# Value product of two local-attention models with the values as the loaded operand

## The chip, the cores and the metric

The kernel runs on one core of one Trainium2 chip. The metric is the device time of one execution in microseconds, as the median of the runs shown. The core has TensorE (PE, whose weight loads are shown apart as PEld), VectorE (DVE), ScalarE (ACT), GpSimd (POOL) and SyncE (SP), which issues the DMAs.

## The reference, cut to what matters

The network is a chain of four parts: a chunked attention, a first local-attention model (six layers, 16 heads, window 32), a causal linear attention, and a second local-attention model (two layers, 8 heads, window 64), each with its normalisations and residuals. The change touches the local attention, which both models share. Per head, with w the window and 64 features:

```python
bq = q.reshape(b, h, nw, w, d)
bk2, bv2 = (look(bk), look(bv))        # own window and the one before: 2w keys
sim = jnp.einsum('bhwie,bhwje->bhwij', bq, bk2) * QK_SCALE
sim = jnp.where(mask, -jnp.finfo(sim.dtype).max, sim)
attn = jax.nn.softmax(sim, -1)
out = jnp.einsum('bhwij,bhwje->bhwie', attn, bv2)
...
return out @ Wo
```

Everything is computed in fp32. There are 4096 tokens of width 128 (two batches of 2048).

## The kernel before, in words

After a first stage of about 600 us (the chunked attention, `l0_attention`), `local_models` runs both local models as one sequence of tiles. A tile is 128 tokens of one batch in one layer: 6 layers x 32 = 192 tiles of the first model (W = 32, four windows to a tile, 16 heads), then 2 x 32 = 64 of the second (W = 64, two windows, 8 heads). The linear attention lies beside the last layers as small steps (`lsteps`), and each layer's feed-forward as steps of 512 tokens (`steps`).

The loop at line 1471 is a software pipeline written out by hand. Each engine executes its instructions in the order of this loop. In iteration i, with j = i + 3:

1. `scores(i+1)` (line 974), then the exponential and the row sums (`weights_exp`, `weights_norm`),
2. `project(j, 0)` (line 862): queries and keys by TensorE (L871), squares on ACT (L873), rotary products on DVE (L881, L886) with a sum on POOL (L892), and in the last unit the norms on DVE (L897 and `rsqrt_quick`, ending in rq_y at L180) and two scalings on POOL (L904),
3. a feed-forward step, then `keys_first_(i)` (line 1023), which transposes the attention weights to pT (keys on partitions; L1030, copied by ACT at L1031), then the rest of the projection,
4. `mix(i)` (line 1034): the value product (L1047), copied by ACT to `on` (L1053),
5. `values(i+2)` (line 943): the values by TensorE (L955), copied by ACT (L956), and DMAs that lay them out as v2 with 2W keys on partitions,
6. `turn_out(i)` (line 1056): `on` is transposed by TensorE (L1063) and copied by ACT to oT (L1064), which has features on partitions,
7. `turn(i+2)` (L936): queries and keys are transposed,
8. a feed-forward step, then `project_out(i)` (line 1067): oT times Wo (L1075), and the residual by DVE (L1081).

PSUM is held as two buffers of two banks (`wide`: projection and scores) and a ring of four single banks (`bank`: everything else). The scratch of `rsqrt_quick` lies in the projection's own PSUM buffer, so that this buffer comes free when rq_y is done.

The small products of scores and of the value product use parts of the 128x128 array. In `scores` a head's 64 features take half of the rows (q = 0 or 1 chooses the half), a window's W queries are the loaded columns, and the 2W keys are streamed. In `mix` the 2W keys of a window are the rows (half of the array for W = 32, chosen by s; all of it for W = 64), a window's W queries are the loaded columns (pT), and the 64 features of v2 are streamed; the output has queries on partitions.

The pieces of the trace are read by these line numbers. The trace has two records for each fp32 matmul and for each of its loads.

Of the kernel before, what the change touches and what calls it, by code (L numbers as in the profile page):

```python
# [11 lines left out]
F32 = mybir.dt.float32  # L12
# [60 lines left out]
def tile_kernel(ctx: ExitStack, tc: tile.TileContext, a: dict, out: bass.AP):  # L73
    nc = tc.nc
# [26 lines left out]
    def bc(ap, shape):  # L101
        return ap.to_broadcast(list(shape))

    ident = const.tile([128, 128], F32, name="ident")
# [603 lines left out]
    def local_models(mA, mB, hs0):  # L708
# [3 lines left out]
        wk = ctx2.enter_context(tc.tile_pool(name="f_k", bufs=1))  # L712
# [4 lines left out]
        def wide(name):  # L717

            return psA.tile([128, 1024], F32, tag="A", name=f"ps_{name}")

        def bank(name):
            return psT.tile([128, 512], F32, tag="T", name=f"ps_{name}")
# [50 lines left out]
        layers = [(m, l) for m in models for l in range(m.depth)]  # L773
        tiles = [(g, b, t) for g in range(len(layers)) for t in range(NTILE) for b in range(B)]
        n, per = len(tiles), B * NTILE
        st = [dict() for _ in range(n)]
# [4 lines left out]
        def load_proj(g, u):  # L781

            m, l = layers[g]
            w = wpool.tile([128, 1024], F32, tag="wp", name="wp", bufs=4)
            c = u * 1024
            k = min(1024, 3 * m.INNER - c)
            nc.sync.dma_start(w[:, 0:k], a[f"{m.pre}_ffn_Wqkv"][l, :, c:c + k])
            wts[g, u] = w
# [185 lines left out]
        def scores(i):  # L974

            g, b, t = tiles[i]
            m, _ = layers[g]
            W, H, HPG = m.W, m.H, m.HPG
            qT, kT = st[i].pop("q"), st[i].pop("k")
            sp = wide("s")  # L980
            for q in range(2):


                rows, sel, j = (slice(0, 128), identb, 0) if t == 0 else (
                    slice(64 * q, 64 * q + 64), pick, 1)
                nc.tensor.matmul(
                    sp[:, 512 * q:512 * q + 512], lhsT=sel[rows],
                    rhs=bc(m.maskb[rows, j].unsqueeze(1), (rows.stop - rows.start, HPG, 2 * W)),
                    start=True, stop=False,
                )  # L990
            for cc in range(HPG):
                for q in range(2):
                    for w in range(m.NW):
                        c0 = 512 * q + 2 * W * cc
                        nc.tensor.matmul(  # L995
                            sp[W * w:W * w + W, c0:c0 + 2 * W],
                            lhsT=qT[64 * q:64 * q + 64, cc, W * w:W * w + W],
                            rhs=kT[64 * q:64 * q + 64, cc, W * w:W * w + 2 * W],
                            start=False, stop=(cc == HPG - 1),
                        )  # L1000
            v = lambda x: x.rearrange("p (h k) -> p h k", k=2 * W)
            mx = wk.tile([128, 16], F32, name="mx")
            nc.vector.tensor_reduce(mx[:, 0:H], v(sp), AX.X, ALU.max)  # L1003
            sm = wk.tile([128, 1024], F32, name="sm", bufs=2)
            nc.vector.tensor_tensor(
                v(sm), v(sp), bc(mx[:, 0:H].unsqueeze(2), (128, H, 2 * W)), ALU.subtract
            )
            st[i]["p"] = sm

        def weights_exp(i):  # L1010
            sm = st[i]["p"]
            nc.scalar.activation(sm, sm, AF.Exp)  # L1012

        def weights_norm(i):
            m, _ = layers[tiles[i][0]]
            sm = st[i]["p"]
            v = sm.rearrange("p (h k) -> p h k", k=2 * m.W)
            rs = wk.tile([128, 16], F32, name="rs", bufs=2)[:, 0:m.H]
            nc.vector.tensor_reduce(rs, v, AX.X, ALU.add)  # L1019
            nc.vector.reciprocal(rs, rs)  # L1020
            nc.gpsimd.tensor_tensor(v, v, bc(rs.unsqueeze(2), (128, m.H, 2 * m.W)), ALU.mult)  # L1021
# [11 lines left out]

        def mix(i):

            m, _ = layers[tiles[i][0]]
            W, NO = m.W, m.NO
            pT, v2 = st[i].pop("pT"), st[i].pop("v")
            po = [bank("o") for _ in range(NO)]
            on = wk.tile([128, 2, 4, 128], F32, name="on")  # L1040
            for c in range(4):
                for s in range(NO):
                    kp = slice(2 * W * s, 2 * W * (s + 1))
                    for q in range(2):
                        co = 128 * c + 64 * q
                        for w in range(m.NW):
                            nc.tensor.matmul(  # L1047
                                po[s][W * w:W * w + W, co:co + 64],
                                lhsT=pT[kp, q, c, W * w:W * w + W],
                                rhs=v2[kp, w, co:co + 64], start=True, stop=True,  # L1050
                            )
            for s in range(NO):
                nc.scalar.copy(on[:, s].rearrange("p c i -> p (c i)"), po[s])  # L1053
            st[i]["on"] = on

        def turn_out(i):
            m, _ = layers[tiles[i][0]]
            on = st[i].pop("on")
            oT = wk.tile([128, 2, 4, 128], F32, tag="pT", name="oT")
            for s in range(m.NO):  # L1060
                p = bank("oT")
                for c in range(4):
                    nc.tensor.transpose(p[:, c * 128:(c + 1) * 128], on[:, s, c, :], ident)  # L1063
                nc.scalar.copy(oT[:, s].rearrange("p c i -> p (c i)"), p)  # L1064
            st[i]["o"] = oT

        def project_out(i):
# [21 lines left out]
        def step():  # L1089
            if steps:  # L1090
                steps.pop(0)()
# [4 lines left out]
        def lstep():  # L1096
            if lsteps:
                lsteps.pop(0)()
# [372 lines left out]
        for i in range(-3, n):  # L1471
            j = i + 3
            lstep()
            if 0 <= i + 1 < n:
                scores(i + 1)
                weights_exp(i + 1)
                weights_norm(i + 1)
            more = False
            if j < n:
                g, b, t = tiles[j]  # L1480
                jj = j % per
                nu = len(layers[g][0].units)
                more = g < last
                if g == second and t % 4 == 0:
                    while (b, t // 4) not in ready:
                        lstep()
                if nu == 2:
                    project(j, 0)
                if more and jj == 4:
                    load_proj(g + 1, 0)  # L1490
                if more and jj == 6 and g + 1 == second:
                    models[1].consts()
                if jj == 6 and g == second - 1:
                    linear_consts()
                if more and jj == 8:
                    factors(g + 1)
                    if 2 == 2:
                        load_out(g + 1)
                if more and jj == 18:
                    load_ff(g + 1)  # L1500
                if more and jj == 22:
                    fold_ff(g + 1)
                if nu == 2 and more and jj == per - 1:
                    load_proj(g + 1, 1)
                lstep()
            step()
            if i >= 0:
                keys_first_(i)
            if 0 <= i + 2 < n:
                halo(i + 2)  # L1510
            if j < n:
                project(j, nu - 1)
                if nu == 2 and more and jj == per - 1 and g + 1 < second:
                    load_proj(g + 1, 2)
                if nu == 1 and more and jj == per - 1:
                    load_proj(g + 1, 1)
                if b == B - 1 and j + 1 < n:
                    tables(*tiles[j + 1][::2])
            lstep()
            if i >= 0:  # L1520
                mix(i)
            lstep()
            if 0 <= i + 2 < n:
                values(i + 2)
            lstep()
            if i >= 0:
                turn_out(i)
            if 0 <= i + 2 < n:
                for u in range(len(layers[tiles[i + 2][0]][0].units)):
                    turn(i + 2, u)  # L1530
            step()
            lstep()
            if i >= 0:
                g, b, t = tiles[i]
                project_out(i)
                if 2 == 1 and i % per == per - 1 and g < last:
                    load_out(g + 1)
                if t % 4 == 3:
                    feed_forward(g, b, t // 4)
# [74 lines left out]
```

## Time and profile before

| what | value |
|---|---|
| runs | 4997.42, 5001.14, 5006.03 us; median 5001.14 |
| the profiled execution | 5004.26 us |
| its span | 5002.5 us |
| granted TensorE clock, mean | 0.961 |
| PE matmul records / PEld records | 74820 / 74850 |
| value product L1047 | 26624 records: 24576 of form 64*32 64x64, 2048 of form 128*64 128x64 |
| scores L995 | 26624 records: 24576 of form 64*32 64x64, 2048 of form 64*64 64x128 |
| transposes of the outputs L1063 | 1792 records |

A form such as "64*32 64x64" means 64 rows and 32 loaded columns of the array, with 64 partitions and 64 columns streamed. In a group of the profile, "busy" is the time in which at least one of its instructions was in flight, followed by the mean duration of one in ns; behind the bar stands the idle time of the engine just before them, and what ended it. In the timeline a row gives the start, the length, the engine, the line, the form and the number of records. In the chain that ended last a row gives the start, the length, and what held the chain.

### The profile page before, as it was taken

Reading aid. Unit: us, or ns where it says so; the run is one execution under the profiler, and the core shown is the slowest. Engines: PE = TensorE matmul, PEld = TensorE weight load, DVE = VectorE, ACT = ScalarE, POOL = GpSimd, SP = SyncE. Lnnn points to the kernel's source line nnn. Section 1 sums busy time; section 2 is a strip of 40 time slices with the busy share of each in tenths; the row PEclk is TensorE's granted clock in tenths of the full one; section 3 lists DMA queues with packets and bytes.
Section 4 is the critical chain, followed back from the end, with each engine's and each line's share of the span. In section 5 each row is a group of like instructions: output and inputs, shape, how many; then the busy total and the mean of one; then the engine's idle time right before and its main releaser. Section 6 shows DMA issues by size and latency. Waiting matters only on the chain.

```text
span 5002.5 us, 170719 instructions
## 1 busy us (share of the span) xinstructions
PE 4572.7 (91%) x74820; PEld 3143.2 (63%) x74850; DVE 3973.1 (79%) x6840; ACT 2883.5 (58%) x4665; POOL 2780.8 (56%) x1666
## 2 busy tenths in 40 slices
PE   5667799999999999999999999999999989899897
PEld 4445566666666666666666666666666666555554
DVE  6993488888888888888888888888877777787885
ACT  3233366666666656666666666666555555565564
POOL 3332366666666666666666666666555544455452
PEclk8778899999999999999999999999999999999999
DMA  2000322222222322223222322232222211111111
GB/s 77 1 1 25 84 69 67 63 72 74 71 64 63 83 71 63 63 76 76 66 66 64 83 67 64 65 78 73 54 55 52 63 45 38 39 46 40 53 53 37
DMA packets 222487, 295.59 MB, mean 59 GB/s; under 512 B 75656, under 2 KB 95408, under 8 KB 221744
## 3 DMA queue, kind: packets, MB, share of 16 engines
q1 hardware_dynamic: 221744, 284.67, 22.0%
q8 instruction: 590, 9.67, 0.8%
q14 instruction: 153, 1.25, 0.1%
HBM read 40.98 MB, written 10.75 MB: 10 GB/s over the span
## 4 chain that ended last, share of the span: by engine, by line
PE 53%; DVE 20%; ACT 8%; POOL 5%; issue 3%; DMA 1%; SPq 0%; POOLq 0%; ACTq 0%; DVEq 0%
PE ps_qk L871 11%; PE ps_v L955 6%; PE ps_f L1158 5%; PE ps_turn L936 5%; PE ps_y L1075 5%; PE ps_o L1047 5%; PE ps_s L995 4%; DVE ps_qk L897 4%; POOL r L892 3%; DVE t L886 3%; PE ps_fy L1183 3%; PE ps_oT L1063 3%; ACT sq L873 2%; DVE r L881 2%; PE ps_pT L1030 2%
## 5 line engine op out<-in xcount | busy, mean ns | idle before, releaser
L892 POOL TENSOR_TENSOR r<-r,t 128x1024 f32<-128x1024 f32 x448 | 1061.2, 2369 | 995.9 <-DVE t L886 770.5
L904 POOL TENSOR_TENSOR r<-r,rq_y 128x1024 f32<-128x1024 f32 x448 | 844.0, 1902 | 455.9 <-DVE rq_y L180 439.2
L873 ACT ACTIVATE sq<-ps_qk 128x1024 f32<-128x1024 f32 x448 | 460.4, 1028 | 1006.4 <-PE ps_qk L871 999.9
L871 PE MATMUL ps_qk<-wp,hs 128*128 128x512 f32 x1792 | 884.4, 615 | 68.3 <-DVE rq_y L180 41.3
L881 DVE TENSOR_TENSOR r<-ps_qk,tb 128x1024 f32<-128x1024 f32 (+1 forms) x512 | 550.1, 1074 | 175.4 <-ACT sq L873 166.9
L886 DVE TENSOR_TENSOR t<-ps_qk,tb 128x1024 f32<-128x1024 f32 (+1 forms) x512 | 553.2, 1080 | 145.0 <-POOL r L892 144.5
L1021 POOL TENSOR_TENSOR sm<-sm,rs 128x1024 f32<-128x1024 f32 x256 | 487.2, 1903 | 263.3 <-DVE rs L1020 172.3
L897 DVE TENSOR_REDUCE ps_qk<-sq 128x16 f32<-128x1024 f32 x448 | 549.1, 1226 | 12.3
L1047 PEld LDWEIGHTS ps_o<-v,pT 64*32 64x32 f32 (+1 forms) x26624 | 356.8, 109 | 289.1 <-ACT pT L1031 175.7
L871 PEld LDWEIGHTS ps_qk<-wp,hs 128*128 128x128 f32 x1792 | 306.7, 191 | 326.2 <-issue 235.6
L955 PE MATMUL ps_v<-wp,hs 128*128 128x512 f32 x896 | 471.9, 639 | 1.0 <-ACT on L1053 0.6
L1047 PE MATMUL ps_o<-v,pT 64*32 64x64 f32 (+1 forms) x26624 | 418.1, 224 | 59.6 <-ACT pT L1031 32.7
L1075 PEld LDWEIGHTS ps_y<-oT,wo 128*128 128x128 f32 x3584 | 429.2, 192 | 48.0 <-issue 42.2
L936 PE MATMUL ps_turn<-ident,r 128*128 128x128 f32 x3584 | 443.2, 276 | 13.3 <-POOL r L904 11.8
L1075 PE MATMUL ps_y<-oT,wo 128*128 128x128 f32 x3584 | 446.3, 276 | 1.8 <-ACT oT L1064 1.8
L936 PEld LDWEIGHTS ps_turn<-ident,r 128*128 128x128 f32 x3584 | 405.7, 143 | 19.8 <-POOL r L904 16.6
L1003 DVE TENSOR_REDUCE mx<-ps_s 128x16 f32<-128x1024 f32 (+1 forms) x256 | 312.9, 1222 | 110.8 <-PE ps_s L995 107.4
L995 PE MATMUL ps_s<-kT,qT 64*32 64x64 f32 (+1 forms) x26624 | 371.6, 230 | 0.4
L1019 DVE TENSOR_REDUCE rs<-sm 128x16 f32<-128x1024 f32 (+1 forms) x256 | 310.3, 1212 | 68.6 <-ACT sm L1012 67.5
L1158 PE MATMUL ps_f<-fx,w 128*128 128x512 f32 (+1 forms) x768 | 356.4, 600 | 1.7 <-DVE fx L1141 1.7
L995 PEld LDWEIGHTS ps_s<-kT,qT 64*32 64x32 f32 (+1 forms) x26624 | 321.3, 107 | 57.1 <-issue 46.2
L956 ACT COPY vn<-ps_v 128x512 f32<-128x512 f32 x448 | 262.5, 586 | 112.3 <-PE ps_v L955 93.4
(268 smaller groups left out, 7554.6 us busy)
## 6 DMA issues: line engine op xcount, KB each, us to landing
v<-vn SPq DMA_DIRECT2D x1276, 128.0 KB
v<-vn SPq DMA_DIRECT2D x744, 64.0 KB
v<-vn SPq DMA_DIRECT2D x64, 256.0 KB
wp<-in_L_ffn_Wqkv SPq DMA_DIRECT2D x20, 512.0 KB
xD<-xb SPq DMA_DIRECT2D x24, 256.0 KB
xb<-xD SPq DMA_DIRECT2D x24, 256.0 KB
cs<-in_cos SPq DMA_DIRECT2D x128, 32.0 KB
cs<-in_sin SPq DMA_DIRECT2D x128, 32.0 KB
```

What stands on the lines that cost most here:

```text
L871: nc.tensor.matmul(pq[:, js], lhsT=hw, rhs=wts[g, u][:, js], start=True, stop=True)
L881: nc.vector.tensor_tensor(r[:, es].rearrange("p (h d) -> p h d", d=DH), pq[:, es].rearrange("p (h d) -> p h d", d=DH), bc(tb[:, 0, s].unsq ...
L886: nc.vector.tensor_tensor(t2[:, es].rearrange("p (h s d) -> p h s d", s=2, d=32), pq[:, es].rearrange("p (h s d) -> p h s d", s=2, d=32)[: ...
L892: nc.gpsimd.tensor_tensor(r, r, t2, ALU.add)
L897: nc.vector.tensor_reduce(pq[:, 16 * v:16 * v + 16], st[i].pop(("sq", v)).rearrange("p (h d) -> p h d", d=DH), AX.X, ALU.add,)
L904: nc.gpsimd.tensor_tensor(rv, rv, bc(y[:, 16 * v:16 * v + 16].unsqueeze(2), (128, 16, DH)), ALU.mult)
L936: nc.tensor.transpose(p[:, c * 128:(c + 1) * 128], r[:, cs], ident)
L955: nc.tensor.matmul(p, lhsT=hw, rhs=wv, start=True, stop=True)
L995: nc.tensor.matmul(sp[W * w:W * w + W, c0:c0 + 2 * W], lhsT=qT[64 * q:64 * q + 64, cc, W * w:W * w + W], rhs=kT[64 * q:64 * q + 64, cc, W ...
L1047: nc.tensor.matmul(po[s][W * w:W * w + W, co:co + 64], lhsT=pT[kp, q, c, W * w:W * w + W], rhs=v2[kp, w, co:co + 64], start=True, stop=True,)
L1075: nc.tensor.matmul(py[:, 0:128], lhsT=wts[g, "o"][:, c * NO + s, :], rhs=oT[:, s, c, :], start=(c + s == 0), stop=(c == 3 and s == NO - 1),)
L1158: nc.tensor.matmul(ps_[c][0:sz], lhsT=wts[g, "w1"][:, o:o + sz], rhs=S["x"], start=True, stop=True,)
```

## The change

In `mix` the two operands change places: the values (v2, 2W keys by 64 features) are loaded, and the attention weights (pT, 2W keys by W queries) are streamed. The output then has features on partitions: the two heads of a pair (q) go to the two column halves of the array, and the result is what `turn_out` made. `turn_out` and its call are removed, and the copy by ACT writes oT, which gets a buffer of its own in place of `on` (before, it shared pT's). The loops are ordered so that, for W = 32, consecutive matmuls go to the four quarters of the array in turn (s the row half, q the column half). In `scores` the two inner loops change places, so that consecutive matmuls alternate between the row halves.

```diff
--- before.py
+++ after.py
@@ -989,8 +989,8 @@
                     start=True, stop=False,
                 )
             for cc in range(HPG):
-                for q in range(2):
-                    for w in range(m.NW):
+                for w in range(m.NW):
+                    for q in range(2):
                         c0 = 512 * q + 2 * W * cc
                         nc.tensor.matmul(
                             sp[W * w:W * w + W, c0:c0 + 2 * W],
@@ -1033,35 +1033,25 @@
 
         def mix(i):
 
+
             m, _ = layers[tiles[i][0]]
             W, NO = m.W, m.NO
             pT, v2 = st[i].pop("pT"), st[i].pop("v")
             po = [bank("o") for _ in range(NO)]
-            on = wk.tile([128, 2, 4, 128], F32, name="on")
+            oT = wk.tile([128, 2, 4, 128], F32, name="oT")
             for c in range(4):
-                for s in range(NO):
-                    kp = slice(2 * W * s, 2 * W * (s + 1))
+                for w in range(m.NW):
                     for q in range(2):
                         co = 128 * c + 64 * q
-                        for w in range(m.NW):
+                        for s in range(NO):
+                            kp = slice(2 * W * s, 2 * W * (s + 1))
                             nc.tensor.matmul(
-                                po[s][W * w:W * w + W, co:co + 64],
-                                lhsT=pT[kp, q, c, W * w:W * w + W],
-                                rhs=v2[kp, w, co:co + 64], start=True, stop=True,
+                                po[s][64 * q:64 * q + 64, 128 * c + W * w:128 * c + W * w + W],
+                                lhsT=v2[kp, w, co:co + 64],
+                                rhs=pT[kp, q, c, W * w:W * w + W], start=True, stop=True,
                             )
             for s in range(NO):
-                nc.scalar.copy(on[:, s].rearrange("p c i -> p (c i)"), po[s])
-            st[i]["on"] = on
-
-        def turn_out(i):
-            m, _ = layers[tiles[i][0]]
-            on = st[i].pop("on")
-            oT = wk.tile([128, 2, 4, 128], F32, tag="pT", name="oT")
-            for s in range(m.NO):
-                p = bank("oT")
-                for c in range(4):
-                    nc.tensor.transpose(p[:, c * 128:(c + 1) * 128], on[:, s, c, :], ident)
-                nc.scalar.copy(oT[:, s].rearrange("p c i -> p (c i)"), p)
+                nc.scalar.copy(oT[:, s].rearrange("p c i -> p (c i)"), po[s])
             st[i]["o"] = oT
 
         def project_out(i):
@@ -1523,8 +1513,6 @@
             if 0 <= i + 2 < n:
                 values(i + 2)
             lstep()
-            if i >= 0:
-                turn_out(i)
             if 0 <= i + 2 < n:
                 for u in range(len(layers[tiles[i + 2][0]][0].units)):
                     turn(i + 2, u)
```

## The prediction

> **What bounds the kernel now.** I read the page's busy line first, then the busy times by stage, the chain that ended last, the groups of the lines that the change edits, and last the instruction timeline, for the pace of TensorE inside each edited stage.
>
> ```profile
> PE 4572.7 (91%) x74820; PEld 3143.2 (63%) x74850; DVE 3973.1 (79%) x6840; ACT 2883.5 (58%) x4665; POOL 2780.8 (56%) x1666
> ...
> PE 53%; DVE 20%; ACT 8%; POOL 5%; issue 3%; DMA 1%; SPq 0%; POOLq 0%; ACTq 0%; DVEq 0%
> ```
>
> ```profile
> core 0: us, PE busy (x) PEld busy (x) DVE busy (x) ACT busy (x) POOL busy (x), PEclk, DMA share, GB/s
> 606.00:4007.00 3401.00, 3292.01 (x62588) 2280.70 (x62590) 2816.40 (x4561) 2121.08 (x3400) 2137.28 (x1249) 0.99 0.27 68
> 4021.00:4950.00 929.00, 835.42 (x7404) 546.60 (x7404) 720.73 (x1520) 542.62 (x820) 451.41 (x291) 0.97 0.16 44
> ```
>
> The two windows run from the first to the last scores matmul of the first local model (192 tiles, 17.8 us each) and of the second (64 tiles). In the first PE is busy 97% and DVE 83%; in the second 90% and 78%. Summing the chain in slices of 100 us, PE holds 2104 of 3217 us (65%) up to 3820 us and 528 of 1179 us (45%) after it. So PE work is the first bound of the first model, and a shared one in the second. This is a stretch of that chain in which only PE works:
>
> ```profile
> 2451.36 1.72 PE ps_qk L871 x4
> 2453.08 1.50 PE ps_o L1047 x104
> 2454.59 1.91 PE ps_v L955 x4
> 2456.50 0.87 PE ps_oT L1063 x8
> 2457.37 1.75 PE ps_turn L936 x16
> ```
>
> Elsewhere the chain leaves PE for a loop: projection L871 (2.0 us), square on ACT (1.0), then on DVE, POOL and DVE again up to rq_y, whose end frees the two-bank buffer for the next projection. One such loop took 15.3 us (2409.62 to 2424.94), some 2 us under a tile's average.
>
> **Pace of the edited stages.** The timeline of PE shows each as a burst; records overlap, so the pace is (bar length less one record) / (records less one).
>
> ```profile
> 2453.01 1.58 PE L1047 MATMUL ps_o<-v,pT 64*32 64x64 f32 x128
> ...
> 2462.05 1.49 PE L995 MATMUL ps_s<-kT,qT 64*32 64x64 f32 x128
> ```
>
> ```profile
> 393.23 1.87 PE L530 MATMUL ps_r<-vt,wt 64*64 64x64 f32 x58 [0.77 <-ACT wt L502]
> ...
> 424.82 1.67 PE L587 MATMUL ps_y<-qT,bx 128*128 128x64 f32 x14
> ...
> 4300.98 1.15 PE L1047 MATMUL ps_o<-v,pT 128*64 128x64 f32 x32
> ...
> 4313.20 1.10 PE L995 MATMUL ps_s<-kT,qT 64*64 64x128 f32 x32
> ```
>
> Every fp32 matmul is two records (26624 for 13312). With a record of 0.22 us, the value product runs at 10.7 ns per record here (median of the bursts 11.0), scores at 10.0, L530 (64 loaded and 64 streamed columns, two column halves of one row half) at 28.9, the second model's value product at 30.0. With 0.27 us, L587 (one tile, 128 loaded, 64 streamed) has 107 ns and the second model's scores (four quarters, 64 loaded, 128 streamed) 26.8, which is 107 ns per quarter.
>
> **Part 1: the transposes go.**
>
> ```profile
> L1063 PE MATMUL ps_oT<-ident,on 128*128 128x128 f32 x1792 | 245.4, 278 | 30.0 <-ACT on L1053 29.6
> L1064 ACT COPY oT<-ps_oT 128x512 f32<-128x512 f32 x448 | 245.0, 592 | 49.1 <-PE ps_oT L1063 49.1
> L1053 ACT COPY on<-ps_o 128x512 f32<-128x512 f32 x448 | 244.7, 588 | 141.8 <-PE ps_o L1047 141.3
> ```
>
> A row of eight takes 0.87 us of PE's path, 109 ns each. First model: 8 records x 192 tiles x 0.109 = 168 us; second: 4 x 64 x 0.109 = 28 us. PE also idled 30 us before them for the copy of `on`, all of it in the second model (the first model's waits show none). ACT loses 448 copies, 245 us; it holds under a tenth of the chain, so I take nothing for that beyond the wait. The remaining copy now writes oT itself: same bytes, same duration. oT has a buffer of its own, so the next pT copy no longer waits for the output projection; no such wait is among PE's, so nothing is taken. Two PSUM banks fewer per tile are asked of the ring of four. `turn` comes 0.87 us earlier; its POOL input L904 ended several us before it in the tiles I looked at (PE waits for it 12 us in all), so that cover holds.
>
> **Part 2: the value product with 64 loaded and 32 streamed columns.** First model only: 128 records a tile as before, but over four quarters instead of eight tiles, so 32 records to a quarter. No row shows 64 loaded with 32 streamed. The bounds per quarter: if streaming set the pace, 32 columns at the 53 ns per 64 columns of the scores rows are 27 ns, plus the 5 ns that L530 shows above 53: 32 ns, a burst of 32 x 32 = 1.0 us. If loading sets it, L530's 58 ns stays, a burst of 1.87 us. L587 decides: there too the load is twice the stream, and the pace is 107 ns where the stream alone is 53; half of that is 54. Quarters side by side don't disturb each other: the second model's scores run four quarters with 64-column loads at the full streaming pace. I take 58 ns: 1.87 us against 128 x 11.0 = 1.41, so **+0.46 us** a tile, 88 us in 192 tiles. In the second model load (128x64) and stream (64) keep their sizes and the column halves alternate as before: nothing, and nothing below it, since neither size nor sequence of tiles differs.
>
> A rule speaks against this part. The Trainium skill, "TensorEngine Tiling (Array Packing)", section "Instruction Overhead", says that a matmul costs about 60 cycles even with one streamed column, and that no gain is to be had from a dimension that is already small. At the 2.4 GHz that the skill's "TensorE: Matmul & The Clock Gate" gives in its first table, 60 cycles are 25 ns (an estimate; the granted clock here is 0.99); 128 records would be 3.2 us before and after, the product's cost would not move, and neither would scores': the sum below would be 161 us instead of 125. The rows of 10.7 and 10.0 ns say that this price isn't paid per instruction when tiles run side by side; I keep the rows.
>
> **Part 3: scores with rows alternating.** Same instructions, other order. In the record starts, each row half issues one per 16.7 ns, then pauses about 60 ns after some 16, because eight records for one half stand ahead of the other's eight. Two halves without pauses are 8.33 ns per record: 128 x (10.0 - 8.33) = 0.21 us a tile, 41 us. Bounds: 0 (if the pauses come from elsewhere) and 0.35 us (if the pace falls to the 58 ns per tile of L530, 7.3 ns per record); a loss is excluded, as neither half gets more work. I take 0.21. In the second model scores already run at streaming pace: nothing.
>
> **Sum.** First model: -168 - 41 + 88 = -121 us of PE work. What counts is between PE's share of the chain, 65%, and all of it, as PE is 97% busy; the loop of 15.3 us catches the shorter tiles, so I take three quarters: -90 us. Second model: transposes 28 plus waits 30 are 58 us; the chain carries L1063 with 31 us, and the copy behind it is then late next with DVE's softmax line; I take -35 us (from 15 to 58). Together -125 us. The profiled execution took 5004.26 us (span 5002.5 and 1.8 around it): 4879; the median of the runs is 3.1 lower, so **4876 us**. With the ends of the two shares (65 to 100%, 15 to 58 us) this case alone spans 4820 to 4908.
>
> **Rivals.** (a) *The DVE loop takes over*: DVE has 14.7 us a tile, and if the loop rather than PE sets nearly every tile, PE's freed time becomes waiting of L871 for rq_y (35 us now). For: the 35% of the chain off PE. Against: PE is 97% busy, and such waits are 1%. Taking 25% in the first model and 15 us in the second, -45 us: 4956. (b) *Loads hide*: the quarter runs at 32 ns, the product shrinks to 1.0 us, and the first model loses 168 + 41 + 77 = 286 us of PE work, of which with the loop near 65% count: -186 - 35, so 4780. L587 speaks against it. (c) *Slower: loads of the two column halves of a row half queue up.* "TensorE: Matmul & The Clock Gate" (Part 3, The mechanism) lets a load overlap running matmuls only where the row group differs. In L530 loads start 2 to 3 ns after a matmul of the same row half, which contradicts it for 256 records; but there streams were as long as loads. If 64-column loads queue at 53 ns, a row half's 64 records take 3.41 us, +2.0 us a tile; the first model gains 168 + 41 and loses 384, all on PE's path, and with the second model's 35 the sum is +140: 5141. It ends slower than before once the product's burst passes 2.7 us (21 ns per record), where the loss eats the transposes, the scores and the second model's gain.
>
> **Chances.** Main case 0.60; (a) 0.18, a third of which ends within 0.2% of before; (b) 0.07; (c) 0.15. A difference of 0.2%, 10 us, is about what a measurement of this kernel can tell. So faster 0.79, same 0.06, slower 0.15. The range reaches from (b) to past (a), 4775 to 4985, and leaves out (c) and the tails.
>
> **What would show it.** Right: no L1063 and L1064; the value product as 64*64 64x32 at about 14.6 ns per record and 1.9 to 2.1 us a tile; scores at 8.3 to 9 ns; PE busy down by about 170 us; ACT by 245; more waits of L871 for rq_y. Wrong: a product burst over 2.7 us or near 1.0, scores still at 10, or PE's work down as computed but its waits up by as much.

## The result, and the profile after

The changed kernel takes 4989.3 us (median of 7 runs, 4985.3 to 4994.4) against 5005.2 us for the kernel before (7 runs): a ratio of 0.9972, 95% interval 0.9961 to 0.9983. By the ratio it is 14 us faster, where 125 were forecast, and its median is 4 us above the upper end of the range. The sign was right, the size was not.

The page of the changed kernel, busy times and chain:

```profile
PE 4522.4 (91%) x73028; PEld 3080.9 (62%) x73058; DVE 3949.9 (79%) x6840; ACT 2641.9 (53%) x4207; POOL 2783.4 (56%) x1666
...
PE 47%; DVE 25%; ACT 7%; POOL 6%; issue 4%; DMA 1%; SPq 0%; POOLq 0%; DVEq 0%; ACTq 0%
```

ACT lost its 245 us, as forecast. PE lost 50 us of busy time, not some 170, and the chain moved from PE (53% to 47%) to DVE (20% to 25%). The edited groups (busy, mean ns | idle before), first in the kernel before, then in the changed one:

```profile
L1047 PE MATMUL ps_o<-v,pT 64*32 64x64 f32 (+1 forms) x26624 | 418.1, 224 | 59.6 <-ACT pT L1031 32.7
...
L995 PE MATMUL ps_s<-kT,qT 64*32 64x64 f32 (+1 forms) x26624 | 371.6, 230 | 0.4
```

```profile
L1048 PE MATMUL ps_o<-pT,v 64*64 64x32 f32 (+1 forms) x26624 | 532.1, 221 | 36.5 <-ACT pT L1031 19.9
...
L995 PE MATMUL ps_s<-kT,qT 64*32 64x64 f32 (+1 forms) x26624 | 384.1, 231 | 0.3 <-issue 0.3
```

To see PE's path as a whole, I gave each record the time to the start of the next one (or to its own end, and the rest as idle), and summed by the name of the product's tile (the rows take in the first stage's products of the same name, which don't change). Before, then after, in us:

```
                      busy                 idle ahead of it
value product         503.7 -> 611.2         104.6 ->  81.3
transposes of outputs 204.9 -> 0           30.0 ->   0
scores, first model   287.9 -> 296.8            0.4 ->   0.3
projection q, k       839.3 -> 850.6          68.3 -> 110.0
turn                  401.6 -> 408.4          13.3 ->  40.4
all of PE            4572.3 -> 4521.9        417.8 -> 455.3
```

The value product costs 107 us more where 88 were forecast. Where nothing stands inside the burst its pace is 14.6 to 15.0 ns per record, as computed; this burst has (2.07 - 0.22) / 127, which is 14.6:

```profile
2440.47 2.07 PE L1048 MATMUL ps_o<-pT,v 64*64 64x32 f32 x128
```

Scores give nothing back. And the idle time ahead of the projection and of `turn` grows by 69 us. The waits of PE name whom they wait for (us in all, times, longest), before and after the change:

```profile
PE ps_qk L871 <- DVE rq_y L180: 41.3, 56, 3.7
...
PE ps_qk L871 <- DVE sm L1005: 16.9, 34, 3.0
PE ps_turn L936 <- POOL r L904: 11.8, 11, 2.3
```

```profile
PE ps_qk L871 <- DVE rq_y L180: 82.6, 82, 3.7
...
PE ps_turn L936 <- POOL r L904: 36.9, 16, 3.5
```

(The prediction's "35 us now" is the first of these in a stretch of the first model.) A stretch of the chain shows what is late instead. Between two projections it runs through ACT, DVE and POOL only:

```profile
2516.74 2.00 PE ps_qk L871 x4
2518.76 1.04 ACT sq L873
2519.83 1.23 DVE r L881
2521.05 1.12 DVE rs L1019
2522.18 1.14 DVE t L886
...
2523.45 2.37 POOL r L892
2525.84 1.23 DVE t L886
...
2533.28 0.20 DVE rq_y L180
2533.53 3.07 PE ps_qk L871 x4
```

This is the loop that the prediction had described. It takes 16.8 us here, of which PE works 2.

**The granted clock fell too**, and neither the prediction nor the experiments below reckoned with it. The mean over the span was 0.961 before and is 0.956 after. The second model in the changed kernel, from its first to its last scores matmul (after the length of the window come the busy times from PE to POOL; the clock is third from the end):

```profile
4008.00:4940.00 932.00, 826.55 (x7155) 531.51 (x7153) 718.93 (x1525) 498.17 (x748) 454.53 (x292) 0.95 0.16 44
```

The clock was 0.97 there before. In the 89 runs of the kernel before that were made beside the experiments, at clocks from 0.957 to 0.965, each 0.001 less goes with 3.3 us more (correlation -0.89). An estimate from this: 0.005 less clock stands for some 17 us, and at the clock of before the change would have given about 31 us instead of 14. No run holds the clock still, so this is an association and not a cause shown. (One run of experiment 2, at a granted clock of 0.811, took 5320 us and is left out of its ratio.)

### The profile page after: what moved, and what is told of

Its sections match the earlier page's. It is cut to its first block, busy times and chain, and to the rows that moved or that the text cites. A ratio compares the mean times of both kernels' runs of the same rounds, so it can differ in the third digit from the quotient of the medians.

```text
span 4990.3 us, 166474 instructions
## 1 busy us (share of the span) xinstructions
PE 4522.4 (91%) x73028; PEld 3080.9 (62%) x73058; DVE 3949.9 (79%) x6840; ACT 2641.9 (53%) x4207; POOL 2783.4 (56%) x1666
## 4 chain that ended last, share of the span: by engine, by line
PE 47%; DVE 25%; ACT 7%; POOL 6%; issue 4%; DMA 1%; SPq 0%; POOLq 0%; DVEq 0%; ACTq 0%
PE ps_qk L871 11%; PE ps_o L1048 5%; PE ps_f L1148 5%; DVE ps_qk L897 5%; PE ps_v L955 5%; DVE t L886 5%; PE ps_turn L936 4%; POOL r L892 4%; PE ps_y L1065 4%; PE ps_s L995 3%; DVE r L881 3%; PE ps_fy L1173 3%; DVE rs L1019 2%; ACT sq L873 2%; PE ps_pT L1030 2%
## 5 line engine op out<-in xcount | busy, mean ns | idle before, releaser
L871 PE MATMUL ps_qk<-wp,hs 128*128 128x512 f32 x1792 | 894.9, 622 | 110.0 <-DVE rq_y L180 82.6
L1048 PEld LDWEIGHTS ps_o<-pT,v 64*64 64x64 f32 (+1 forms) x26624 | 479.4, 136 | 309.5 <-ACT pT L1031 162.4
L1048 PE MATMUL ps_o<-pT,v 64*64 64x32 f32 (+1 forms) x26624 | 532.1, 221 | 36.5 <-ACT pT L1031 19.9
L871 PEld LDWEIGHTS ps_qk<-wp,hs 128*128 128x128 f32 x1792 | 310.5, 193 | 367.6 <-issue 236.5
L955 PE MATMUL ps_v<-wp,hs 128*128 128x512 f32 x896 | 482.2, 640 | 1.1 <-ACT oT L1054 0.8
L1054 ACT COPY oT<-ps_o 128x512 f32<-128x512 f32 x448 | 243.8, 588 | 276.0 <-PE ps_o L1048 275.2
L995 PE MATMUL ps_s<-kT,qT 64*32 64x64 f32 (+1 forms) x26624 | 384.1, 231 | 0.3 <-issue 0.3
```

What stands on the lines that cost most here:

```text
L871: nc.tensor.matmul(pq[:, js], lhsT=hw, rhs=wts[g, u][:, js], start=True, stop=True)
L955: nc.tensor.matmul(p, lhsT=hw, rhs=wv, start=True, stop=True)
L995: nc.tensor.matmul(sp[W * w:W * w + W, c0:c0 + 2 * W], lhsT=qT[64 * q:64 * q + 64, cc, W * w:W * w + W], rhs=kT[64 * q:64 * q + 64, cc, W ...
L1048: nc.tensor.matmul(po[s][64 * q:64 * q + 64, 128 * c + W * w:128 * c + W * w + W], lhsT=v2[kp, w, co:co + 64], rhs=pT[kp, q, c, W * w:W * ...
```

## The experiments

Two theories stood against each other. LOOP: the time is set by chains of nearly one length, one through PE and one through ACT, DVE and POOL to rq_y, so that PE work taken away turns into waiting. PRICE: PE is the bound, and the change only costs more PE work than forecast. All ratios are against the kernel before on the same chip, with 95% intervals.

**1. Scores alone.** The kernel before with only the loop order of scores changed:

```diff
-                for q in range(2):
-                    for w in range(m.NW):
+                for w in range(m.NW):
+                    for q in range(2):
```

> The kernel before with only the two inner loops of scores exchanged (rows alternate). My prediction priced this at 41 us of PE work saved, three quarters of it in time: about 30 us faster, 4975. Theory PRICE (PE still sets the time; the stages cost otherwise than forecast; in the changed kernel the first model's scores take 297 us of PE's path against 288 before): 10 to 15 us slower, about 5018. Theory LOOP (PE's freed time turns into waits for DVE's and POOL's loop): within 5 us of before, whichever way PE's work goes. The pace of the bursts should be 10.7 ns per record (PRICE) and not 8.3.

Measured: 1.0003 (0.9993 to 1.0014). Neither my 30 us nor the 10 to 15 us of PRICE; LOOP's "within 5 us" holds. The timeline of the burst shows why; it is as long as before, 1.48 us against 1.49 for 128 records:

```profile
2513.64 1.48 PE L995 MATMUL ps_s<-kT,qT 64*32 64x64 f32 x128
```

The starts of the single records agree with those of before to a few ns through the whole burst, with the same pauses. So the pauses that I had read as the effect of eight records in a row for one row half don't come from that order; where they come from stays open. The slower scores bursts of the changed kernel (1.6 to 1.8 us beside 1.48) occur in the kernel before too, only less often.

**2. The rest of the change alone.** The changed kernel with the scores loops as before:

```diff
-                for w in range(m.NW):
-                    for q in range(2):
+                for q in range(2):
+                    for w in range(m.NW):
                         c0 = 512 * q + 2 * W * cc
```

> The changed kernel with the loops of scores as before (so: transposes gone, value product exchanged). PRICE: the 15 us of scores come back, 4975. LOOP: within 5 us of the changed kernel, 4989. My prediction: 30 us slower than the changed kernel, 5020.

Measured: 0.9984 (0.9975 to 0.9993), which overlaps the changed kernel's interval. The 15 us of PRICE didn't come back: with the old order, the first model's scores took as long (295 us of PE's path, 297 in the changed kernel). LOOP's "within 5 us" holds for the medians, 4992.5 and 4989.3.

**3. The transposes taken away at no price.** In the kernel before, the output projection reads the untransposed copy:

```diff
-            st[i]["on"] = on
+            st[i]["o"] = on
...
-            if i >= 0:
-                turn_out(i)
```

> The kernel before without the transposition of the outputs: the output projection reads the untransposed copy, so what is computed lacks that transposition; everything else stays. It takes 205 us of PE work and 30 us of PE's wait off and adds nothing. PRICE (PE is the bound, about three quarters of it counts): 150 to 200 us faster, 4800 to 4855. LOOP: most turns into waits of the projection for rq_y and of turn for POOL: 40 to 80 us faster, 4925 to 4965.

Measured: 0.9904 (0.9890 to 0.9918), **48 us** for 235 us of PE's path. That lies in LOOP's range. PE's waits in this kernel:

```profile
PE ps_qk L871 <- DVE rq_y L180: 131.6, 86, 4.3
...
PE ps_turn L936 <- POOL r L904: 39.2, 16, 3.7
...
PE ps_qk L871 <- DVE sm L1005: 29.1, 32, 3.4
```

Against 41.3, 11.8 and 16.9 us for these three lines before: 130 us more of waiting, 90 of them for rq_y. From the first to the last scores record the first model takes 3341.7 us (3401.6 before), the second 929.3 (928.5). So in the second model, where the prediction took 35 us, the whole removal of 58 us of PE's work and waits gives nothing; in the first 60 of 168.

Waiting is not all of it. PE's busy time fell by 161 us (4572.7 to 4411.5) where 205 us of work had gone: what is left of PE's work took 44 us longer. The granted clock is 0.951 here. The part of it that was not granted, summed over the time in which PE is busy, is 201 us, against 163 us before, so some 38 of the 44 us are the clock's (an estimate). By the 3.3 us per 0.001 above, the removal at the clock of before would have given some 81 us, a third of 235 and not a fifth. Where PE idles most, the clock is lowest: 0.933 and 0.922 with PE 85% and 84% busy (experiments 7 and 8), 0.918 and 0.905 with 82% and 81% (14 and 13).

Experiment 2 less experiment 3 is the price of the exchanged product: 0.9984 - 0.9904 = 0.0080, 40 us of time for 107 us of PE's path.

**4. A values matmul inside the product.** The text ahead of the prediction says that each engine executes in the order of the loop. For the local models that is wrong: a scheduler orders each engine's instructions at build. In the kernel before it put values into the value product in 25 of the first model's tiles, in the changed kernel in 85, right after the second matmul; the third needs pT's second half, which ACT copies later. This kernel orders the first column group by halves:

```diff
             for c in range(4):
-                for w in range(m.NW):
-                    for q in range(2):
+                wq = [(w, q) for w in range(m.NW) for q in range(2)]
+                if c == 0:
+                    wq.sort(key=lambda x: x[1])
+                for w, q in wq:
```

> As e2, but in the first of the four column groups the eight products of q = 0 stand ahead of those of q = 1. The order in which PE executes is made by a scheduler when the kernel is built; in the changed kernel it puts a values matmul into the value product after its second matmul in 85 of 192 tiles (25 before), since the third needs pT's second half. Here it splits 3 of 192. If the splits cost ([...]the output's copy later): 15 to 30 us faster than e2, 4950 to 4960. If they don't: equal to e2, or up to 10 us slower, since 32 records run on two quarters instead of four.

Measured: 0.9998 (0.9988 to 1.0007), not faster than experiment 2. The product itself took 42 us more of PE's path (656 against 614): 32 of its records run on two quarters here. The splits' price, if any, is no more than what this costs.

**5 and 6. The buffer freed early, scratch in SBUF.** The prediction's loop ends at rq_y because the scratch lies in the projection's PSUM buffer. Both kernels with the following (an unused constant is removed to make room)

```diff
+                sc4 = wk.tile([128, 4, 32], F32, name="rq_s")
...
-                        pq[:, 16 * v:16 * v + 16],
+                        sc4[:, 0, 16 * v:16 * v + 16],
...
-                y = rsqrt_quick([pq[:, k * 32:k * 32 + 2 * H] for k in range(4)], 2 * H, wk)
+                y = rsqrt_quick([sc4[:, k, 0:2 * H] for k in range(4)], 2 * H, wk)
```

> The kernel before, with the scratch of rsqrt_quick in SBUF instead of in the projection's PSUM buffer (an unused constant makes room). The buffer then comes free when the second rotary product has been read (L886), some 5 us before rq_y. If this buffer is the link by which DVE's loop holds PE, waits of L871 for rq_y (41 us) go and the time falls by 20 to 50 us, 4950 to 4980; if the link is elsewhere (DVE's and POOL's work itself), within 10 us of before.

> The changed kernel with the same move of the scratch. If the buffer is the link that swallowed the change's gain, PE's saved work counts now, and this run is 40 to 70 us under e5, at 4900 to 4930. If the distance between the two stays at the 14 us of the change, the gain is lost to something else than this buffer.

Measured: before with it 1.0070 (1.0056 to 1.0084), the changed kernel with it 0.9956 (0.9943 to 0.9969). The distance is 56 us, which is in the range of the buffer as the link; the levels missed, and experiment 5 is slower where it was to be faster. PE's wait of L871 for rq_y is down to 1.7 us in both, but DVE became 154 and 165 us busier. The first operation on the scratch, its group in the kernel before, in PSUM, and in experiment 5, in SBUF:

```profile
L167 DVE TENSOR_SCALAR ps_qk<-ps_qk 128x32 f32<-128x32 f32 (+1 forms) x256 | 49.2, 192 | 7.0
```

```profile
L165 DVE TENSOR_SCALAR rq_s<-rq_s 128x32 f32<-128x32 f32 (+1 forms) x256 | 221.9, 867 | 5.7
```

So this pair shows that the change's worth depends on what else binds, and isn't a clean test of the buffer.

**7 and 8. Program order.** Both kernels with the scheduler's order switched off in the local models (one line after the pools):

```diff
+        ctx2.enter_context(tc.manual_schedule())
```

> The kernel before with both local models in program order on every engine (the order is otherwise made by the scheduler at build). Without a scheduler that fills gaps it may be slower or faster by up to 3%; it is the base for e8 and says nothing alone.

> The changed kernel in program order: no values matmul stands inside a value product. If the scheduler's other order swallowed the gain, e8 is 60 to 120 us under e7. If PE's freed time turns into waits for DVE, POOL and ACT whatever the order, e8 is 10 to 30 us under e7.

Measured: 1.1133 (1.1118 to 1.1147) and 1.1130 (1.1116 to 1.1144). In an order in which PE idles 845 us, the change is worth nothing that can be told: PE's busy time falls by 35 us, its idle time rises by 31, and the clock falls from 0.933 to 0.922. The 3 us are below both expected ranges; they speak against the scheduler's other order as the thief, and fit LOOP.

**9, 10 and 11. DVE's part made shorter.** The norms are summed over 8 of each head's 64 squares, in the kernel before, in the changed one, and in that of experiment 3:

```diff
-                        st[i].pop(("sq", v)).rearrange("p (h d) -> p h d", d=DH), AX.X, ALU.add,
+                        st[i].pop(("sq", v)).rearrange("p (h d) -> p h d", d=DH)[:, :, 0:8], AX.X, ALU.add,
```

> The kernel before, with the norms on DVE summed over 8 of each head's 64 squares (what is computed lacks the rest): some 430 of DVE's 549 us at L897 go, which lie in DVE's loop from projection to rq_y; PE's work stays. LOOP (time is set by the chain from projection through ACT, DVE and POOL to rq_y as much as by PE): 100 to 200 us faster, 4800 to 4900, more per us taken away than the removed transposes gave. PRICE (PE is the bound, 97% busy): at most 30 us faster, since PE's work stays.

> The changed kernel with the same lighter norms. LOOP: with DVE's part shorter, PE's saved work counts, and this run is 35 to 80 us under e9 where the change alone gave 14. If the distance stays at 14 us or less, the change's saving is not held back by DVE's part of the chain.

> The kernel before without the transposition of the outputs (as e3, left out) and with the lighter norms of e9. LOOP: 110 to 190 us under e9, where the same removal alone gave 48. If it stays near 48, PE's removed work is hidden by something else than DVE's norms.

Measured against the kernel before, with DVE as it is and with the lighter norms (us worked out from the ratios or medians):

```
                       DVE as it is               lighter norms
kernel before            0                        0.9876 (0.9857 to 0.9895)   -62
the change             0.9972   -14               0.9708 (0.9687 to 0.9729)  -146
transposes removed     0.9904   -48               0.9503 (0.9482 to 0.9524)  -249
```

Between the rows of the right column the change is worth 84 us, six times as much, and the removal 187 us, which is 0.8 of its 235 us and not 0.2. PE's busy time fell by 190 us in the removal (4569 to 4380) and not by 161. The clock hardly differs in the right column (means of the runs 0.960, 0.959, 0.959), so it can account for some 28 of the 139 us between 48 and 187 (the same estimate); the rest goes with DVE's part. The busy times and the chain of experiment 10, the changed kernel with lighter norms:

```profile
PE 4507.6 (93%) x73058; PEld 3075.0 (63%) x73058; DVE 3576.7 (73%) x6840; ACT 2650.3 (54%) x4217; POOL 2775.7 (57%) x1666
...
PE 66%; DVE 11%; ACT 6%; POOL 3%; issue 2%; DMA 1%; SPq 0%; POOLq 0%; DVEq 0%; ACTq 0%
```

PE has 66% of the chain where it had 47%, and the wait for rq_y is down from 82.6 us:

```profile
PE ps_qk L871 <- DVE rq_y L180: 16.2, 25, 1.9
```

The expectation for experiment 9, 100 to 200 us, was too high: removing 355 us of DVE's work (3973.1 to 3618.5) alone gave 62, and PRICE's "at most 30 us" was too low. So DVE alone isn't the bound either. Taking 235 us of PE's path gives 48 us, taking DVE's work 62, both together 249, more than twice the sum of the two.

**12. PE's work added.** Each transposition of the outputs done twice in the kernel before:

```diff
-                for c in range(4):
+                for c in list(range(4)) * 2:
                     nc.tensor.transpose(p[:, c * 128:(c + 1) * 128], on[:, s, c, :], ident)
```

> The kernel before with every transposition of the outputs done twice into the same bank: about 196 us of PE work more, nothing else. Taking this work away gave 48 us. LOOP as a balance of two chains of nearly one length predicts that adding PE work costs much more of its size than removing it gives: 110 to 200 us slower, 5115 to 5205. If PE's work were covered by DVE's part over a wide span, adding would cost as little as removing gives, 40 to 60 us.

Measured: 1.0265 (1.0245 to 1.0285), 132 us for 197 us more of PE's path: 0.67 of it counts. Taken away, 0.20 of 235 us counted.

**13 to 16. The buffer freed early, scratch in PSUM.** Here DVE's operations stay as they are. First in a bank of the ring of four, then in a bank of its own, with a ring of three:

```diff
+                sp4 = bank("rq")
...
-                        pq[:, 16 * v:16 * v + 16],
+                        sp4[:, 16 * v:16 * v + 16],
```

```diff
-        psT = ctx2.enter_context(tc.tile_pool(name="f_psT", bufs=4, space=PSUM))
+        psT = ctx2.enter_context(tc.tile_pool(name="f_psT", bufs=3, space=PSUM))
+        psR = ctx2.enter_context(tc.tile_pool(name="f_psR", bufs=1, space=PSUM))
...
+                sp4 = psR.tile([128, 512], F32, tag="R", name="ps_rq")
```

> The kernel before with the scratch of rsqrt_quick in a bank of the ring of four. If the projection's buffer is the link, waits of L871 for rq_y (41 us) go. But the ring holds a bank some 5 us longer each tile, in which order it is given out, so pT, values and turn wait for it: 50 us faster to 150 us slower.

> The changed kernel with the scratch in the ring, of which it uses two banks fewer per tile. If the buffer was the link: 30 to 80 us under e13. If DVE's and POOL's work is the link: 10 to 30 us under e13.

> The kernel before with the scratch in a PSUM bank of its own and a ring of three banks. DVE's operations stay as they are. If the buffer is the link: 20 to 60 us faster than before, unless the shorter ring costs as much; if DVE's and POOL's work is the link: within 20 us of before or slower.

> The changed kernel with the scratch in a bank of its own and a ring of three. If the buffer is the link: 40 to 80 us under e15, and with that the fastest of the complete kernels, 4880 to 4940. If the work itself is the link: 10 to 30 us under e15.

Measured: in the ring 1.2106 (1.2088 to 1.2125) and 1.1455 (1.1433 to 1.1478); far outside what was expected of the first. PE's longest wait there is `turn` for rq_y (512 and 316 us), so the ring is the new bound, and the change, with two banks fewer per tile, is worth over 300 us. With a bank of its own 1.0121 (1.0102 to 1.0140) and 0.9964 (0.9951 to 0.9977). Between the last two the change is worth 77 us, for 73 us of PE busy time less, and no wait for rq_y is left among PE's longest. That distance fits the buffer as the link; the levels do not, since experiment 15 is 61 us slower than before and 16 is not under 4940 us. But the ring of three also favours the kernel that asks for two banks fewer, so the two aren't told apart. None of the complete kernels is faster than the changed one beyond the intervals (0.9956 and 0.9964 beside 0.9972).

## Why the prediction was wrong

**The step that failed** is the one from PE's work to time: "What counts is between PE's share of the chain, 65%, and all of it, as PE is 97% busy [...] so I take three quarters". Experiment 3 measures it: 0.20 over the kernel, 0.36 in the first model (60 of 168 us), nothing in the second, where "I take -35 us". A share of the chain tells how much of the time PE's work holds now. It does not tell how much of that is given back when the work goes, for the other chain lies just behind: the prediction's own loop of 15.3 us, "some 2 us under a tile's average", is one loop out of many, and PE already waited for rq_y 56 times; in the changed kernel it waits 82 times, in experiment 3 86. The prediction also put at nothing that the rest of PE's work would run at a lower clock. And "97% busy" was no evidence for PE: with 168 us of its work gone from the first model, PE still is 94% busy there, 3142.93 of 3342 us:

```profile
605.00:3947.00 3342.00, 3142.93 (x61103) 2124.82 (x61094) 2794.21 (x4560) 1929.79 (x3020) 2137.12 (x1247) 0.98 0.27 69
3961.00:4890.00 929.00, 820.97 (x7141) 532.22 (x7132) 713.74 (x1518) 498.21 (x746) 452.34 (x290) 0.95 0.16 44
```

(experiment 3, the first and the second model; the clock is 0.98 and 0.95 there, and was 0.99 and 0.97). The Trainium skill warns of busy time in "Trainium Kernel Development and Optimization", section "Performance Expectations": matmul busy time is a bad measure of how close a kernel is to the limit of the hardware, since matmuls are pipelined, and one of the two measures that it names instead is the load's busy share, which was 67% in the first model before (2281 of 3401 us). Of a second chain it says nothing.

**Part 1**, the transposes: the work that goes was right (205 us and 30 us of waits, against 196 and 30), and ACT's 245 us too. In time: -48 us, where three quarters of 168 and some 35 were taken.

**Part 2**, the exchanged product: right in its mechanism. 58 ns per quarter, 14.6 ns per record; the path grew by 107 us, not 88. In time +40 us (experiments 2 and 3). The rule of 60 cycles that the prediction weighed, 25 ns by its estimate, was set against single records; a matmul is two of them. So counted, the changed product has 29 ns per matmul, which does not speak against the rule; the scores with 20 and the product before with 21 do. The prediction was right to drop the rule, since the product did get dearer.

**Part 3**, scores: wrong. "41 us" are 0 (experiment 1): the pauses don't come from the order of the rows. The lower of the two bounds that the prediction gave, 0, was the value.

**Sum in time**: -48 + 40 + 0 = -8, against -14 +- 5 measured for the whole change. (The first two are experiment 2 by their making, so the sum tests the zero alone.)

**The rivals.** (a), the loop takes over, is what happened; its 25% was near the 20% measured over the kernel, and its -45 us was too large since it kept the scores' 41 us and 15 us in the second model. Its "against" ("such waits are 1%") was the mistake: a wait that is short now does not tell how much slack the second chain has. (b) and (c) are out: the quarters ran at 58 ns.

**What stays open**: where the pauses in the scores come from; what the change would give at an unchanged clock; whether the projection's buffer or the length of DVE's and POOL's work is the link; and what the scheduler's splits cost.

## What to carry to other kernels

In this kernel two chains of nearly one length set the time. Work taken from PE alone gave back a fifth, part of the rest being lost to a lower granted clock; work added to it cost two thirds; work taken from both gave more than twice the sum. So price a saving by removing the work alone, not by the busy share of the engine or its share of the chain, and compare the granted clocks of the two profiles before reading their busy times. The exchange of operands was priced by its load: quarters of the array with 64 loaded columns ran at 58 ns per record whether 64 columns were streamed (L530) or 32 (the changed product).

## What the runs showed of the hardware that was not expected

The first rsqrt operation on scratch in SBUF (128x32, DVE) took 867 ns in the mean, up to 2373, where it takes 192 in PSUM. Of its 256 runs in experiment 5, 191 lasted over 400 ns; every one of these began while a POOL operation ran and ended some 37 ns (median) after a POOL operation's end. The Trainium skill ("SBUF — State Buffer", section "SBUF: two separate sides") says that DVE and GpSimd share a port pair, and that a DVE operation in a mode that uses two ports and a GpSimd operation take it as a lock for a whole instruction, so that the later one blocks. The rows look like that, though the trace doesn't show the mode. So scratch in PSUM isn't neutral: here it kept this operation clear of POOL.
